# A chunked linear recurrence: the key product taken from the state two chunks back plus (k k') times the values between

## The chip, the core and the metric

The kernel runs on one NeuronCore of a Trainium2 chip. The metric is device time in microseconds from one launch to its end, the median of three runs. The profile shows one further execution. The engines are named as the profile names them: PE (matrix products), DVE (VectorE), ACT (ScalarE), POOL (GpSimd), SP (the DMA queue).

## The reference

A transformer layer on x of 2048 tokens and 512 features, all in fp32: a recurrent attention, then a gated FFN, each with a layernorm before and after and a residual sum. The recurrence has 16 heads of 32 and runs over 128 chunks of 16 tokens. Its state S is 32x32 for each head:

```
def step(S, (qi, ki, vi, ei)):                    # one chunk, all heads
    kh     = ki @ S
    mu, rstd = mean(kh), rsqrt(var(kh) + EPS);  kh_hat = (kh - mu) * rstd
    gw     = (w * kh_hat + b - (vi - ki)) * w
    v_new  = (gw - mean(gw) - kh_hat * mean(gw * kh_hat)) * rstd
    A      = tril(qi @ ki.T) * ei
    o      = qi + ln(qi @ S - A @ v_new)
    S      = S - (ki * ei).T @ v_new
    return S, o
```

Before it q = silu(x Wq), k = x Wk with each head's rows normalised, v = x Wv, e = 2 sigmoid(x Wbeta). After it o is gated with sigmoid(x Wg1 Wg2), normalised by head, and multiplied by Wo. The FFN has 1536 inner features; its weights are rounded to fp8 values inside the kernel.

What the change uses: with S_i = S_(i-1) - (k_(i-1) e_(i-1))' v_(i-1), the product k_i S_i is k_i S_(i-1) minus (k_i k_(i-1)') times (e v)_(i-1). The matrix k_i k_(i-1)' needs keys alone.

## The kernel before

**Blocks and steps.** The tokens are worked in 16 blocks of 128 (`NB`), each holding 8 chunks (`NC`) in two halves (`NHALF` = 4). The code counts blocks from 0.

**One step of the recurrence** (the function `chain`), for a chunk i of block b:

- PE, L768: `kh` = k·S, four matmuls whose weights are a spread copy of the keys, `kb` (each head's keys in its own rows and columns, zeros elsewhere), and whose data is `S`. In the trace each fp32 matmul appears as two passes, so a group of four is "x8".
- DVE, L772 to L782: products of `kh` with the rows of `row` (weights, targets) and their sums `z`, which hold mean and variance.
- ACT, L786: a square root. DVE, L790 to L815: a chain of small operations that makes factors and `m`. ACT, L801: part of the result, into a tile `up`'s bank (named u in the code).
- DVE, L821 and L824: `vb`, the new values times -e.
- PE, L832: `up` = `kr`' `vb`, the step of the state, with `kr` the keys in another layout that come back from memory.
- DVE, L840: `S` = `S` + `up`, into SBUF. Then the next step's L768.

Each `vb` also goes to memory (`give`), so that a whole block of values comes back as `vbt`.

**Around it.** For each block `pre` makes the layernorm, the transpose of x (`turned`), k (`product` with `wk_s`, L429, normalised by `head_rsqrt`), the transposed keys `kt` and the spread keys `kb` (L479, four copies on ACT of 32x512 from PSUM). `pre_v` makes v and the targets `tg` on POOL; they go through memory into `row`. `pre_sig` makes q (L583), the gate and beta with sigmoids on ACT (L591 to L599; a sigmoid and a square root need different tables, so that a table load stands between them). `scores` makes q k' (L634) and its mask (POOL, L647). `post` makes the output of a block from `S` of its start, the scores and `vbt`, and the product with `wo_s`. `weights` rounds the FFN's weights in 36 parts on DVE, POOL and ACT. All these are the side work of the recurrence. After its end the FFN runs (L978, L1007).

**The order.** `Sched` is a planner inside the kernel: each piece of work is a generator that yields the engine and the expected time of its next operation. The planner writes the operations out in the order in which they would run, the recurrence first, and lets a side operation stand ahead of a step of the recurrence only if by its costs it ends no later than `SLACK` after the step is due (`need`). On the chip each engine then runs its own list strictly in that order. The due times come from the list `steps`:

```
steps = [
    ("PE", 0.45), ("DVE", 0.4), ("DVE", 0.33), ("DVE", 0.47), ("ACT", 0.28, "sqrt"),
    ...
    ("PE", 0.66), ("DVE", 0.31),
]
```

Of the kernel before, what the change touches and what calls it, by code (L numbers as in the profile page):

```python
# [9 lines left out]
F32 = mybir.dt.float32  # L10
# [3 lines left out]
ALU = mybir.AluOpType  # L14
# [44 lines left out]
R_W = 1.0  # L59
R_PRE, R_SCO, R_POST = 0.0, 0.2, 1.4  # L60
# [20 lines left out]
class Sched:  # L81
# [62 lines left out]
    def run(self):  # L144
        while True:
# [13 lines left out]
            for eng in self.engine:  # L159
# [3 lines left out]
                    if t["chain"] or eng not in need or s + self._us(t) <= need[eng] + self.SLACK[eng]  # L163
# [17 lines left out]
def op(eng, us, need=None, late=0.0, table=None):  # L181
    return ("op", eng, us, need, late, table)
# [3 lines left out]
def kernel(  # L186
# [79 lines left out]
    with ExitStack() as st1:  # L266
# [42 lines left out]
        for n in range(2):  # L309
# [18 lines left out]
            zs.append(t)  # L328
        nums = p_kh.tile([P, D], F32, tag="kh", name="kh")
        kh = nums[:, 0 : 2 * DH].rearrange("p (r e) -> p r e", r=2)  # L330

# [4 lines left out]
        gen, tables = Slots(5), Slots(1)  # L336
# [11 lines left out]
        front = [Event() for _ in range(NB)]  # L348
        kr_in = [Event() for _ in range(2 * NB)]
        data = [{n: Event() for n in ("last_ot", "stored", "scored", "beta", "qt_in")} for _ in range(NB)]  # L350
# [14 lines left out]
        def head_rsqrt(src, scale, tag, newton=False):  # L365

            yield op("ACT", 0.65)
            sq = b2.tile([P, D], F32, tag="sq", name="sq")
            act(sq, src, AF.Square)
            yield op("DVE", 0.73)  # L370
            ss = small.tile([P, NH], F32, tag=tag + "s", name="ss")
            nc.vector.tensor_reduce(ss, by_head(sq), AX.X, ALU.add)
            if newton:
                return (yield from rsqrt_parts(ss, [P, NH], scale, 1e-6, small, tag + "n"))
# [33 lines left out]
        def turned(src, dst):  # L408

            yield ("take", gen, 1)  # L410
            yield op("PE", 0.6)
# [9 lines left out]
        def product(lhs, rhs, name):  # L421
# [3 lines left out]
            for k in range(4):  # L425
                yield op("PE", 1.0)
# [5 lines left out]
        def pre(b):  # L432
# [5 lines left out]
            if b >= 1:  # L438
                yield ("wait", front[b - 1])
# [6 lines left out]
            yield from turned(xn, xt)  # L446
            d["xt"] = xt
            got_k = Event()
            sched.add(pre_sig(b, xt), rank=b + R_PRE + 0.1)
# [22 lines left out]
            yield op("ACT", 0.65)  # L472
            kt = b2.tile([P, 4, P], F32, tag="kt", name="kt")
            nc.scalar.copy(kt, pt)
            d["kt"] = kt
            for h in range(4):
                end = yield op("ACT", 0.6)
                sl = slice(32 * h, 32 * h + 32)
                nc.scalar.copy(  # L479
                    kbs[b % 2][sl, :, :, h * CH : (h + 1) * CH].rearrange("p n g c -> p g n c"),  # L480
                    pt[sl].rearrange("p g (n c) -> p g n c", c=CH),
                )
            gen.put(end)
            ready[b].set(end)
            yield ("wait", d["stored"])
            yield ("wait", d["scored"])
            made[b].set(end)

# [15 lines left out]
        def pre_v(b, xt, got_k):  # L504
# [17 lines left out]
            m = small.tile([P, NH], F32, tag="tm", name="tm")  # L522
# [30 lines left out]
        def pre_sig(b, xt):  # L553
# [4 lines left out]
            for k in range(4):  # L558
                yield op("PE", 0.28)
                if pg is None:  # L560
                    pg = p_gen.tile([P, P], F32, tag="gen", name="pg")
                nc.tensor.matmul(pg[0:64, :], lhsT=wgb_s[:, k, :], rhs=xt[:, k, :], start=(k == 0), stop=(k == 3))
            end = yield op("ACT", 0.3)
            gb = b1.tile([64, P], F32, tag="gb", name="gb")
            nc.scalar.copy(gb, pg[0:64, :])
            gen.put(end)
            if b >= 1:
                yield ("wait", data[b - 1]["scored"])
            if b >= 3:
                yield ("wait", done[b - 3])  # L570
            yield ("take", gen, 3)
            yield op("PE", 0.28)
            pb = p_gen.tile([P, NH], F32, tag="gen", name="pb")
            nc.tensor.matmul(pb, lhsT=gb, rhs=bsel[0:64, :], start=True, stop=True)
            yield op("PE", 1.0)
            pgt = p_gen.tile([P, D], F32, tag="gen", name="pgt")
            nc.tensor.matmul(pgt, lhsT=gb, rhs=wg2_s, start=True, stop=True)
            pq = None
            for k in range(4):
                yield op("PE", 1.0)  # L580
# [4 lines left out]
            sb = b2.tile([P, NH], F32, tag="sb", name="sb")  # L585
# [4 lines left out]
            yield op("ACT", 0.65, table="sig")  # L590
            act(sg, pgt, AF.Sigmoid)  # L591
            end = yield op("ACT", 0.3, table="sig")
            act(sb, pb, AF.Sigmoid)
# [583 lines left out]
```

## Time and profile before

| | |
|---|---|
| median of 3 runs | 1137.34 us (1133.26 to 1147.24) |
| the profiled execution | 1126.66 us |
| its span | 1124.7 us |
| PE busy | 900.9 us, 80% |
| DVE busy | 709.5 us, 63% |
| ACT busy | 557.2 us, 50% |
| POOL busy | 462.4 us, 41% |
| PE's granted clock, mean | 0.838 |

How to read the profile's lines. A timeline line gives start and duration in us, the engine, the line of the kernel, the operation with output and inputs, and in brackets how long the engine stood idle before it and what ended that. PEld is PE's loading of weights, which overlaps its matmuls. A line by stretches gives the stretch and its length, then for PE, PEld, DVE, ACT and POOL the busy time and the number of instructions, then PE's granted clock as a share of full speed, the share of time that the DMA engines were busy, and GB/s. Buffer numbers are left out of names.

### The profile page before, as it was taken

The page shows a single profiled execution, that of the slowest core. Times are in us where ns is not written, and L with a number is a line of the kernel's source. Part 1 is how long each engine was busy: PE and PEld are TensorE (multiplying, and loading weights), DVE is VectorE, ACT ScalarE, POOL GpSimd, SP SyncE. Part 2 cuts the span into 40 slices and gives each one's busy share as a digit, 9 for nine tenths or more (in the row PEclk, how much of TensorE's full clock was granted, in tenths as well). Part 3 has the DMA queues.
Part 4 walks back from the last instruction along what each step waited for, and adds up shares of the span by engine and source line. Part 5 has one row for each costly group of instructions (what it writes and reads, how often), then busy time and mean ns, then how long its engine had stood idle before and what let it go on. Part 6 is the DMA issues. An engine that isn't in the chain of part 4 may idle for free. (4 is left out here: it accounts for less than half of the span.)

```text
span 1124.7 us, 17608 instructions
## 1 busy us (share of the span) xinstructions
PE 900.9 (80%) x5824; PEld 594.8 (53%) x5824; DVE 709.5 (63%) x2418; ACT 557.2 (50%) x1192; POOL 462.4 (41%) x380
## 2 busy tenths in 40 slices
PE   2868877877786877798877988766369999999996
PEld 1434544444443544454444544444236888888885
DVE  2266667667664757766767666676664666476635
ACT  1565546556564646757567575674232223233223
POOL 5543535556544635566545564464441001010011
PEclk9878667887877868886978869876579999999998
DMA  9323121221203222232222322215115001010000
GB/s 312 79 49 78 34 63 39 64 61 46 68 21 102 63 46 48 73 68 53 49 50 69 68 53 58 66 45 150 44 38 227 7 1 38 1 38 1 10 29 37
DMA packets 139370, 68.74 MB, mean 61 GB/s; under 512 B 106640, under 2 KB 119056, under 8 KB 139280
## 3 DMA queue, kind: packets, MB, share of 16 engines
q1 hardware_dynamic: 138256, 66.35, 22.2%
q0 software_dynamic: 272, 0.87, 0.3%
q8 instruction: 46, 0.75, 0.3%
q10 hardware_dynamic: 752, 0.40, 0.1%
q14 instruction: 44, 0.36, 0.1%
HBM read 41.25 MB, written 26.35 MB: 60 GB/s over the span
## 5 line engine op out<-in xcount | busy, mean ns | idle before, releaser
L832 PE MATMUL up<-vb,kr 64*128 64x32 f32 x1024 | 103.0, 313 | 114.8 <-DVE vb L824 72.2
L832 PEld LDWEIGHTS up<-vb,kr 64*128 64x128 f32 x1024 | 90.1, 226 | 178.4 <-ACT up L801 74.7
L978 PE MATMUL gu<-xh,w 128*128 128x512 f32 x384 | 153.2, 399 | 4.2 <-DVE sg L1026 2.4
L978 PE MATMUL gu<-xl,w 128*128 128x512 f32 x384 | 151.8, 395 | 0.0
L1080 POOL TENSOR_TENSOR y<-y,xa 128x512 f32<-128x512 f32 x15 | 19.3, 1288 | 244.9 <-ACT y L1074 171.2
L801 ACT ACTIVATE up<-row,k 128x32 f32<-128x32 f32 x256 | 97.3, 380 | 44.3 <-DVE k L806 28.5
L840 DVE TENSOR_TENSOR S<-S,up 128x128 f32<-128x128 f32 x128 | 36.8, 287 | 115.5 <-PE up L832 115.1
L786 ACT ACTIVATE sk<-z 128x2 f32<-128x2 f32 x128 | 26.0, 203 | 148.7 <-DVE z L782 148.2
L647 POOL TENSOR_TENSOR at<-at,cs 128x512 f32<-128x512 f32 x64 | 80.5, 1279 | 45.0 <-ACT at L640 45.0
L1007 PE MATMUL acc<-w,h 128*128 128x512 f32 x384 | 95.4, 391 | 0.4 <-DVE h L1037 0.2
L429 PE MATMUL pk<-wk_s,xt 128*128 128x512 f32 x128 | 87.9, 823 | 9.0 <-ACT at L640 9.0
L772 DVE TENSOR_TENSOR row<-kh,row 128x192 f32<-128x192 f32 x128 | 45.8, 358 | 71.7 <-PE kh L768 59.5
L768 PE MATMUL kh<-S,kb 128*64 128x32 f32 x1024 | 65.9, 251 | 30.2 <-DVE S L840 27.1
L881 POOL TENSOR_TENSOR raw<-raw,m 128x512 f32<-128x512 f32 x36 | 45.6, 1266 | 97.8 <-DVE m L878 89.9
L978 PEld LDWEIGHTS gu<-xh,w 128*128 128x128 f32 x384 | 73.3, 191 | 20.2 <-DVE sg L1026 2.8
L978 PEld LDWEIGHTS gu<-xl,w 128*128 128x128 f32 x384 | 73.2, 191 | 15.7 <-DVE xl L959 0.4
L1007 PEld LDWEIGHTS acc<-w,h 128*128 128x128 f32 x384 | 72.1, 188 | 16.2 <-ACT h L1035 0.6
L768 PEld LDWEIGHTS kh<-S,kb 128*64 128x64 f32 x1024 | 50.7, 163 | 51.2 <-DVE S L840 43.0
L583 PE MATMUL pq<-wq_s,xt 128*128 128x512 f32 x128 | 77.1, 735 | 0.0
L429 PE MATMUL po<-wo_s,ot 128*128 128x512 f32 x128 | 71.3, 695 | 2.9 <-ACT ot L417 2.9
L1035 ACT CAST h<-sg 128x512 fp32r<-128x512 f32 x48 | 29.9, 623 | 85.2 <-DVE sg L1029 76.7
L429 PE MATMUL pv<-wv_s,xt 128*128 128x512 f32 x128 | 68.1, 650 | 4.9 <-ACT xt L417 3.6
(183 smaller groups left out, 1876.9 us busy)
## 6 DMA issues: line engine op xcount, KB each, us to landing
w8d<-w SPq DMA_DIRECT2D x36, 256.0 KB
w<-w8d SPq DMA_DIRECT2D x12, 768.0 KB
tg_d<-tg SPq DMA_DIRECT2D x32, 132.0 KB
row<-tg_d SPq DMA_DIRECT2D x32, 132.0 KB
kc_d<-kn SPq DMA_DIRECT2D x16, 256.0 KB
kr<-kc_d SPq DMA_DIRECT2D x256, 16.0 KB
vb_d<-vb SPq DMA_DIRECT2D x128, 32.0 KB
vbt<-vb_d SPq DMA_DIRECT2D x16, 256.0 KB
```

The costliest lines, as they stand in the source:

```text
L429: nc.tensor.matmul(pp, lhsT=lhs[:, k, :], rhs=rhs[:, k, :], start=(k == 0), stop=(k == 3))
L583: nc.tensor.matmul(pq, lhsT=xt[:, k, :], rhs=wq_s[:, k, :], start=(k == 0), stop=(k == 3))
L647: gtt(view, view, causal.unsqueeze(1).to_broadcast([P, 4, P]), ALU.mult)
L768: nc.tensor.matmul(kh[half, g // 2, :], lhsT=kb[:, i, g, :], rhs=S[:, g, :], start=True, stop=True)
L772: tt(row[:, :, 3:6, 0:DH], kh.unsqueeze(2).to_broadcast([P, 2, 3, DH]), row[:, :, 0:3, 0:DH], ALU.mult,)
L801: act(u[:, r, :], row[:, r, 4, 0:DH], AF.Identity, bias=k1[:, 0, r : r + 1], scale=k1[:, 1, r : r + 1])
L832: nc.tensor.matmul(up[:, j, r * DH : r * DH + DH], lhsT=kr[half, ii, r, :], rhs=vb[half, r, :], start=True, stop=True,)
L840: tt(S2.rearrange("p (r j) e -> p r j e", r=2), S.rearrange("p (r j) e -> p r j e", r=2), up.rearrange("p j (r e) -> p r j e", r=2), ALU.add,)
L881: gtt(v, raw, m, ALU.add)
L978: nc.tensor.matmul(pp, lhsT=w[:, half, k * P : (k + 1) * P], rhs=part[:, k, :], start=(k == 0 and i == 0), stop=(k == 3 and i == 1),)
L1007: nc.tensor.matmul(accs[tb][s], lhsT=h[:, i, s * P : (s + 1) * P], rhs=w8[f][:, 2, :], start=(f == 0 and i == 0), stop=(f == NF - 1 and i ...
L1035: nc.scalar.copy(h[:, 0, :], sg)
```

## The change

The recurrence no longer needs the newest state for its product. For each pair of neighbouring chunks `gram` makes K = k_(i-1) k_i' from the spread keys (PE, L518, four matmuls a chunk, into one PSUM bank for half a block, copied to SBUF by ACT at L525). In a step k·S (`k_S`, L807) is issued with the state that lacks the newest `vb`, between `m` and `vb`, and leaves its sum open. When `vb` is there, K·vb (L910) is added in PSUM and closes the sum; then `up` (L922) follows. `up` is opened once and summed in PSUM over all 128 chunks, so DVE's sum L840 is gone; instead ACT copies the sum to SBUF as `S` once a step (L847), between `kh`'s first products and the square root.

The spread keys `kb` are written by POOL from `kt` (L491) and no longer by ACT from PSUM. The sigmoid of beta moves: a new `pre_beta` makes its argument early, and `pre_sig` takes block b+1's beta (and block 0's) with block b's gate and q in one run of sigmoids (L646 to L653); `over` lets such a run stand up to `OVER` = 3 us past a due time. Some buffers have one copy instead of two (`sq`, `o`), with slots that guard them. The planner's costs for PE are lower (a product's part 0.88 instead of 1.0), and `steps` holds written start times with a period of 3.94.

```diff
-def op(eng, us, need=None, late=0.0, table=None):
-    return ("op", eng, us, need, late, table)
+def op(eng, us, need=None, late=0.0, table=None, over=0.0):
+    return ("op", eng, us, need, late, table, over)
...
             for h in range(4):
-                end = yield op("ACT", 0.6)
+                end = yield op("POOL", 0.75)
                 sl = slice(32 * h, 32 * h + 32)
-                nc.scalar.copy(
+                nc.gpsimd.tensor_copy(
                     kbs[b % 2][sl, :, :, h * CH : (h + 1) * CH].rearrange("p n g c -> p g n c"),
-                    pt[sl].rearrange("p g (n c) -> p g n c", c=CH),
+                    kt[sl].rearrange("p g (n c) -> p g n c", c=CH),
                 )
...
+        def gram(b, half):
+            n = 2 * b + half
+            if n >= 2:
+                yield ("wait", gram_out[n - 2])
+            yield ("take", gen, 1)
+            pr = None
+            for i in range(NHALF * half, NHALF * half + NHALF):
+                if b == 0 and i == 0:
+                    continue
+                yield op("PE", 0.32)
+                if pr is None:
+                    pr = p_gen.tile([P, NHALF, 2, 64], F32, tag="gen", name="pr")
+                last = kbs[b % 2][:, i - 1] if i else kbs[(b - 1) % 2][:, NC - 1]
+                for g in range(4):
+                    at = slice(64 * (g % 2), 64 * (g % 2) + 64)
+                    nc.tensor.matmul(
+                        pr[at, i % NHALF, g // 2, :], lhsT=last[:, g, :], rhs=kbs[b % 2][:, i, g, :],
+                        start=True, stop=True,
+                    )
+            end = yield op("ACT", 0.65)
+            first = 1 if n == 0 else 0
+            t = b2.tile([P, NHALF, 2, 64], F32, tag="gram", name="gram")
+            nc.scalar.copy(t[:, first:], pr[:, first:])
+            gen.put(end)
+            grams[n % 2] = t
+            gram_in[n].set(end)
...
+            for n in nxt:
+                yield op("ACT", 0.25, table="sig", over=OVER)
+                act(data[n]["sb"], data[n]["sb"], AF.Sigmoid)
+            end = yield op("ACT", 0.65, table="sig", over=OVER)
             act(sg, pgt, AF.Sigmoid)
...
+        def k_S(b, i, S, stop):
+            for g in range(4):
+                half = slice(64 * (g % 2), 64 * (g % 2) + 64)
+                nc.tensor.matmul(
+                    kh[half, g // 2, :], lhsT=kbs[b % 2][:, i, g, :], rhs=S[:, g, :], start=(g < 2), stop=stop and g > 1,
+                )
...
+                    op_S = next(step)
+                    if b or i:
+                        yield ("at", t_up + HOP)
+                        yield op_S
+                        S = state.tile([P, 4, DH], F32, tag="S" if i else "S0", name="S")
+                        nc.scalar.copy(
+                            S.rearrange("p (r j) e -> p r j e", r=2), up.rearrange("p j (r e) -> p r j e", r=2),
+                        )
...
+                        yield ("wait", ready[nb])
+                        yield ("wait", gram_in[n2])
+                        yield op_K
+                        k_S(nb, ni, S, False)
...
+                    t_kh = yield next(step)
+                    for r in range(2):
+                        for j in range(2):
+                            half = slice(64 * j, 64 * j + 64)
+                            nc.tensor.matmul(
+                                kh[half, r, :], lhsT=grams[n2 % 2][half, ni % NHALF, r, :], rhs=vb[half, r, :],
+                                start=False, stop=(r == 1),
+                            )
...
                             nc.tensor.matmul(
                                 up[:, j, r * DH : r * DH + DH], lhsT=kr[half, ii, r, :], rhs=vb[half, r, :],
-                                start=True, stop=True,
+                                start=(b == 0 and i == 0 and r == 0), stop=(r == 1),
+                                skip_group_check=True,
                             )
...
-                    yield next(step)
-                    S2 = state.tile([P, 4, DH], F32, tag="S0" if i == NC - 1 else "S", name="S")
-                    tt(
-                        S2.rearrange("p (r j) e -> p r j e", r=2), S.rearrange("p (r j) e -> p r j e", r=2),
-                        up.rearrange("p j (r e) -> p r j e", r=2), ALU.add,
-                    )
-                    S = S2
```

## The prediction

> **What bounds the kernel now.** I read the granted clock first, then the busy time of each engine by stage, then single steps of the recurrence in the timeline. By stage the trace splits in three:
>
> ```profile
> core 0: us, PE busy (x) PEld busy (x) DVE busy (x) ACT busy (x) POOL busy (x), PEclk, DMA share, GB/s
> 52.00:810.00 758.00, 586.47 (x4415) 349.06 (x4413) 506.57 (x1968) 445.90 (x1012) 394.53 (x322) 0.78 0.25 60
> 810.00:837.00 27.00, 12.42 (x98) 7.11 (x96) 20.09 (x52) 7.44 (x14) 12.71 (x11) 0.69 0.15 41
> 837.00:1124.70 287.70, 275.91 (x1212) 225.19 (x1212) 170.37 (x355) 86.81 (x136) 26.50 (x21) 0.97 0.11 40
> ```
>
> The recurrence owns 758 of 1124.7 us and no engine is full in it: PE 77%, DVE 67%, ACT 59%, POOL 52%, PE's clock only 0.78 on average. The last stage is PE at full clock; the change does not touch it. So the recurrence is bound by its own round trip, 128 times. One step at full clock:
>
> ```profile
> 635.73 0.36 DVE L772 TENSOR_TENSOR row<-kh,row 128x192 f32<-128x192 f32 x1 [0.53 <-PE kh L768]
> ...
> 638.69 0.22 DVE L824 TENSOR_TENSOR vb<-m,up 128x64 f32<-128x64 f32 x1
> ...
> 639.06 0.64 PE L832 MATMUL up<-vb,kr 64*128 64x32 f32 x8 [0.60 <-ACT z L550]
> 639.73 0.29 DVE L840 TENSOR_TENSOR S<-S,up 128x128 f32<-128x128 f32 x1
> ...
> 640.07 0.42 PE L768 MATMUL kh<-S,kb 128*64 128x32 f32 x8
> 640.54 0.36 DVE L772 TENSOR_TENSOR row<-kh,row 128x192 f32<-128x192 f32 x1 [0.53 <-PE kh L768]
> ```
>
> and the same links at half clock:
>
> ```profile
> 803.25 0.22 DVE L824 TENSOR_TENSOR vb<-m,up 128x64 f32<-128x64 f32 x1
> ...
> 803.62 1.07 PE L832 MATMUL up<-vb,kr 64*128 64x32 f32 x8 [3.38 <-ACT m L886]
> 804.72 0.29 DVE L840 TENSOR_TENSOR S<-S,up 128x128 f32<-128x128 f32 x1 [1.25 <-PE up L832]
> ...
> 805.06 0.64 PE L768 MATMUL kh<-S,kb 128*64 128x32 f32 x8 [0.38 <-DVE S L840]
> 805.75 0.36 DVE L772 TENSOR_TENSOR row<-kh,row 128x192 f32<-128x192 f32 x1 [0.75 <-PE kh L768]
> ```
>
> Read each as three parts. A, from the start of `row` (L772) to the end of `vb` (L824): 3.18 us. B, on to the end of `S`: 1.11 us at full, 1.54 at half clock. C, on to the next `row`: 0.52 and 0.74. Over all starts of L772 in the timeline the step takes 5.93 us on average (753.7 us for 127): A 3.48, B 1.64, C 0.81. The floor at full clock is 3.15 + 1.11 + 0.53 = 4.79. The 1.14 us above it come from other work that stands in the way on PE, ACT and DVE, and from half clock, which by the 0.78 holds some 43% of the time (in half-microsecond slices the clock is nearly always 0.5 or 1).
>
> **The change on the round trip.** The new key product K·vb (L910) takes the place of `up`, the sum `S` and k·S after `vb`; k·S itself is issued before `vb` is there. A step is then A plus one matmul group. No row shows that group; the nearest is L768, also eight passes with 64 columns of weights and 32 of data (0.42 us), so its C holds: 0.53 full, 0.75 half clock. Floor: 3.15 + 0.53 = 3.68 us. B leaves the path: 1.1 to 1.5 us a step, 127 times, 140 to 195 us if nothing else were late. What is late next is PE.
>
> **PE's work.** Warm and cold unit times come from the issue intervals of the timeline: a 128x512 product k-step 0.87 and 1.72 us, a k·S group 0.31 and 0.51, an `up` group 0.50 and 0.96, a transpose group 0.46 and 0.80, 16 score or `qh` matmuls 0.9 to 1.8 and 1.6 to 2.0. New are, per chunk, K·vb (0.31 and 0.51) and the making of K (L518; nearest row k·S again, but 64 columns of data: between 0.31 and 0.5, I take 0.34; cold 0.60). With these I add up what PE's issue order holds between two chain groups. Before: 416 us at full clock for 127 steps, 3.28 a step. After: 495 us, 3.93 a step, more than the floor of 3.68. So PE and round trip are now about equal, and half the steps will be set by PE. The order also shows eight places near block ends where 5 to 17 us of other matmuls stand between `up` and the next k·S.
>
> The time of a step I take as the larger of round trip and PE work, at full clock and at half clock, weighted by their shares of time. The round trip is A's mean of 3.48 and the links. With 43% cold, the order of before gives 751 us against the 753.7 measured, so the method needs no correction. The order of after gives 728 us at 43% cold, 690 at 32% (clock 0.84), 648 at 20%, 787 at 60%, 579 with no cold time at all.
>
> **Which clock.** This is the largest choice. The trace:
>
> ```profile
> 478.00:486.00 8.00, 8.00 (x31) 4.68 (x31) 5.46 (x21) 3.36 (x10) 7.06 (x6) 0.50 0.12 31
> ```
>
> PE is busy all 8 us and still at half clock. The Trainium skill (TensorE: Matmul & The Clock Gate, Part 1: The HAM clock gate) says that about 3.4 us of sustained work release the full clock. By that rule the changed kernel, whose PE hardly pauses, runs at 1.0: 579 us. By this row a busy PE of small matmuls and waits is not enough, and the clock stays 0.78: 728 us. The row decides that the rule's "busy" is not the page's busy; but the work per time does rise, from 416/754 = 0.55 to about 0.7, which thins out the slack stretches that precede each drop. I take 0.84, 690 us: **-64 us**.
>
> **ACT.** It loses 64 `kb` copies (L479, 574 ns, 37 us) and, by the order, 28 of 60 table loads (1.283 us each, 36 us), since the sigmoids of two blocks stand together. It gains 127 copies of `S` from PSUM (nearest L474-like copies; 128 elements between 0.2 and 0.4, I take 0.29 as on DVE: 37 us), 32 copies of K (580 ns, 19 us). Net -17 us on an engine 59% busy. Two table loads around a sigmoid hold up the chain's square root (L786) by one to two microseconds; A's excess over 3.15 is 0.33 x 128 = 42 us in all. Half of the groups of loads go, each remaining one is longer: **-8 us** (bounds 0 and -20). The copy of `S` adds a wait: ACT stands until `up` is done, with the square root and both `up` activations (L801) behind it, and `m` waits for these. `up` ends about 0.6 us after `row` starts and the square root is wanted at 1.2, so 0.3 us are left after the copy at full clock; nearly nothing at half clock or with a transpose in between (45 of 127 steps have something there, 20 of them over 0.3 us). I cost it at nothing, bounds 0 and +35.
>
> **POOL and the block ends.** Spreading the keys moves from ACT to POOL, in order between its 1.27 us operations, and now ends in a PE group that waits for it, with the chain behind on PE. A one-input copy of 32x512 has no row: the memset of 128x2048 (1.825 us) scales to 0.46 for 512, the two-input L647 takes 1.27, the slowest, L304, 1.56. The Trainium skill (GPSIMD Engine Reference, 4.1 Engine selection) speaks against elementwise work there, but calls one-input work roughly line-rate. By that about the memset's pace, 64 x 0.5 = 32 us, by L647 81 us; I take 0.8, 51 us, which POOL can hold (395 + 51 of some 695). On the path are only the ends of blocks: four copies, K's making and its copy cost some 4 us instead of 2.3 us, and four blocks (8, 9, 10 and 15 of 0 to 15) have K directly ahead of its use: **+8 us** (0 to +45).
>
> **Start and end.** The first `row` waits for `tg` (L547's transfer, 5.8 us of idle DVE before it). The sigmoid in `tg` now waits for block 1's product and stands on ACT behind both copies of K: about 50 instead of 44 us, **+6 us** (0 to +10). Of the weight roundings one or two more parts remain after the last mask (POOL, 3.8 us each); the FFN needs them some 50 us later. SP's order is the same in kind. The end: no change.
>
> **Sum.** -64 - 8 + 8 + 6 = -58 us on 1126.66 (span 1124.7 plus 2): 1068.7. The median shown, 1137.34, lies 0.95% above the profiled execution; scaled, **1079 us**. About 2% is what a measurement of this kernel can tell from no change.
>
> **Rivals.**
> *Full clock* (0.15). The rule above holds: 10% cold gives about 613 us, total -135: 1001 us. For it: the last stage holds 0.97. Against: the row at 478.
> *Late keys* (0.17). POOL or the K groups hold up each block end by 2 to 3 us more, 15 times: +35, 1114 us. For it: one such stall of 9.4 us (the C ahead of block 6, blocks counted from 0) is in the trace already with ACT doing the copies. Against: POOL has 48% idle.
> *ACT couples the steps* (0.08). The wait for `up` delays the square root by 0.27 us a step: +35, 1114 us.
> *PE becomes the bound and stays cold* (0.10), the slower side. Place: PE's queue between `up` and k·S; price: 79 us more matmul at full clock, 133 at half clock. With the clock at 0.70 the sum is 787: +33 + 6 = +39, 1177 us. It decides from about 49% cold time (clock below 0.755), where the sum passes 748. For it: the added matmuls are all small, the kind present at half clock.
> That the change fails to shorten the path: K·vb waits, by the order, for `vb` alone within a half block; I give it no chance of its own.
>
> The forecast keeps 0.50, with its own range 1035 to 1112. Faster by over 2%: forecast, full clock and half of the two 1114 cases, 0.74; within: 0.19; slower: 0.07. The range that leaves out most of the cold case and the warmest end: 1018 to 1130.
>
> **What would show it.** Right: start to start of `row` near 5.4 us, K·vb to `row` 0.5 to 0.75, A still 3.4 to 3.6, PE busy over 85% and clock 0.80 to 0.88 in the recurrence, table loads 32 there, `kb` on POOL at 0.5 to 1.3 us, last stage 288 us. Wrong: A above 3.8 (ACT or DVE), stalls ahead of the K groups at block ends, or a clock at or below 0.76.

## The result and the profile after

The changed kernel takes **1138.74 us** (median of 20 executions, 1135.83 to 1142.35), the kernel before 1132.77 us, also of 20, in the same comparison: ratio 1.0051, 95% interval 1.0033 to 1.0070. It is half a per cent slower, where 1079 us and a gain of 5% were forecast.

The profiled execution spans 1138.6 us against 1124.7. By stage (the table of windows of the changed kernel: recurrence from the first to the last `row`, the stretch between, the last stage):

```profile
62.80:805.28 742.48, 640.14 (x6352) 402.23 (x6352) 470.54 (x1823) 408.75 (x1081) 418.61 (x369) 0.82 0.25 60
805.28:836.00 30.72, 13.61 (x104) 9.32 (x104) 27.17 (x71) 9.10 (x20) 17.83 (x14) 0.61 0.13 37
836.00:1138.60 302.60, 277.66 (x1212) 226.13 (x1212) 171.31 (x355) 89.80 (x141) 34.32 (x27) 0.96 0.11 41
```

The columns are, as before, length, then busy time of PE, PE's weight loads, DVE, ACT and POOL, then PE's clock. The recurrence gained 11.2 us (753.7 to 742.5). The first `row` starts 10.8 us later (62.8 instead of 52.0), and from the last `row` to the end it takes 14.4 us longer (333.3 instead of 319.0). The sum is the 13.9 us that the span grew.

The step itself became what the change intended. This is one at full clock (the timeline of the changed kernel; L833 is `row`, L807 k·S, L902 `vb`, L910 the new K·vb):

```profile
150.62 0.36 DVE L833 TENSOR_TENSOR row<-kh,row 128x192 f32<-128x192 f32 x1
...
153.30 0.42 PE L807 MATMUL kh<-S,kb 128*64 128x32 f32 x8 [0.99 <-ACT up L872]
...
153.61 0.22 DVE L902 TENSOR_TENSOR vb<-m,up 128x64 f32<-128x64 f32 x1
...
153.88 0.42 PE L910 MATMUL kh<-vb,gram 64*64 64x32 f32 x8 [0.15 <-DVE vb L902]
...
154.35 0.36 DVE L833 TENSOR_TENSOR row<-kh,row 128x192 f32<-128x192 f32 x1
```

k·S is done before `vb` is, and `row` follows `vb` by one matmul group: 3.73 us from `row` to `row`; the shortest step of the trace has 3.68. The median step fell from 5.62 to 4.86 us. But 7 of the 127 steps take 11 to 27 us, 135 us together, where before one took 14. All seven are the last step of a block of eight. This is the one at the end of block 9, 27.2 us (the same view; L885 is `m`, L485 `kt`, L491 the keys' copies, L518 the making of K, L899 and L902 the two adds that end in `vb`):

```profile
513.98 0.29 DVE L885 TENSOR_TENSOR m<-row,kh 128x128 f32<-128x128 f32 x1
...
517.59 0.57 ACT L485 COPY kt<-pt 128x512 f32<-128x512 f32 x1
...
527.92 3.72 POOL L702 TENSOR_TENSOR at<-at,cs 128x512 f32<-128x512 f32 x3 [0.18 <-ACT at L695]
531.60 1.23 POOL L758 TENSOR_TENSOR o<-o,r 128x512 f32<-128x512 f32 x1
532.77 2.75 POOL L491 COPY kb<-kt 32x512 f32<-32x512 f32 x4
...
535.58 0.45 PE L518 MATMUL pr<-kb,kb 128*64 128x64 f32 x8 [0.75 <-POOL kb L491]
...
537.82 0.21 DVE L899 TENSOR_TENSOR up<-m,up 128x64 f32<-128x64 f32 x1
538.07 0.22 DVE L902 TENSOR_TENSOR vb<-m,up 128x64 f32<-128x64 f32 x1
```

`m` is there at 514.3 and `vb`, two short adds later, at 538.3. In between every engine works through side operations. The four key copies were ready at 518.2 and ran at 532.8, behind masks and norms of other blocks; that looks like late keys, and the experiments had to tell whether it is.

The seven are not all held at the same place. In four, at the ends of blocks 2, 3, 11 and 14 (84 of the 135 us), `vb` and K·vb are done within 8 us of the step's `row`, and the next `row` waits: for the load of `tg`, and behind side operations on DVE. The one at the end of block 2, whose own `row` starts at 180.31:

```profile
184.95 0.42 PE L910 MATMUL kh<-vb,gram 64*64 64x32 f32 x8
...
203.78 1.98 SPq L588 DMA_DIRECT2D row<-tg_d  x2
...
207.50 0.36 DVE L833 TENSOR_TENSOR row<-kh,row 128x192 f32<-128x192 f32 x1 [5.05 <-DMA row<-tg_d]
```

The start, in the same view (L525 copies K, L646 is beta's sigmoid, L572 puts beta into `tg`, L588 loads `row`):

```profile
50.00 0.59 ACT L525 COPY gram<-pr 128x512 f32<-128x512 f32 x1 [0.45 <-PE pr L518]
50.59 1.28 ACT L646 ACT_TABLE_LOAD   x1
51.88 0.32 ACT L646 ACTIVATE sb<-sb 128x16 f32<-128x16 f32 x2
...
54.78 0.21 ACT L572 ACTIVATE tg<-sb 128x16 f32<-128x16 f32 x1
...
58.97 1.99 SPq L588 DMA_DIRECT2D row<-tg_d  x2
```

Beta of block 0 waits on ACT behind both copies of K; its column in `tg` is written at 54.8 instead of 44.2. The end, in the same view (the last part of the rounded weights on POOL and its store; then the FFN's cast L1119, its gate L1110 and its matmul L1062):

```profile
884.30 1.26 POOL L975 TENSOR_TENSOR w<-raw,m 128x512 fp32r<-128x512 f32 x1 [1.46 <-issue]
885.59 0.32 SPq L977 DMA_DIRECT2D w8d<-w  x1
...
887.79 0.62 ACT L1119 CAST h<-sg 128x512 fp32r<-128x512 f32 x1 [3.63 <-DMA w8d<-w]
...
889.05 0.75 DVE L1110 SCALAR_TENSOR_TENSOR sg<-gu,ps,sg 128x512 f32<-128x512 f32 x1
...
889.85 0.80 PE L1062 MATMUL gu<-xh,w 128*128 128x512 f32 x1 [12.54 <-DVE sg L1110]
```

The matmul waits for the gate on DVE, the gate for a sigmoid on ACT (L1107, at 888.32), and that stands in ACT's list behind the cast, which starts when the store of the last rounded weights has landed. So the late rounding holds the FFN through ACT's queue. Before, the last rounding on POOL ended at 853 us and the longest wait of PE in the last stage's first 160 us was 2.4 us.

### The profile page after: what moved, and what is told of

It is laid out like the page before. It is cut to its first block, busy times and chain, and to the rows that moved or that the text cites. A ratio compares the mean times of both kernels' runs of the same rounds, so it can differ in the third digit from the quotient of the medians.

```text
span 1138.6 us, 21826 instructions
## 1 busy us (share of the span) xinstructions
PE 964.3 (85%) x7848; PEld 655.1 (58%) x7848; DVE 681.0 (60%) x2290; ACT 524.9 (46%) x1275; POOL 502.4 (44%) x444
## 5 line engine op out<-in xcount | busy, mean ns | idle before, releaser
L1062 PE MATMUL gu<-xh,w 128*128 128x512 f32 x384 | 153.7, 400 | 13.8 <-DVE sg L1110 13.1
L1062 PE MATMUL gu<-xl,w 128*128 128x512 f32 x384 | 152.0, 396 | 2.4 <-DVE xl L1043 2.4
L833 DVE TENSOR_TENSOR row<-kh,row 128x192 f32<-128x192 f32 x128 | 45.9, 358 | 160.0 <-PE kh L910 132.9
L807 PEld LDWEIGHTS kh<-S,kb 128*64 128x64 f32 x1024 | 48.9, 156 | 119.9 <-ACT up L872 73.4
L847 ACT COPY S<-up 128x128 f32<-128x128 f32 x127 | 33.7, 265 | 171.4 <-PE up L922 137.5
L807 PE MATMUL kh<-S,kb 128*64 128x32 f32 x1024 | 62.2, 243 | 59.0 <-ACT up L872 29.4
L922 PE MATMUL up<-vb,kr 64*128 64x32 f32 x1016 | 96.6, 312 | 0.0
L1062 PEld LDWEIGHTS gu<-xh,w 128*128 128x128 f32 x384 | 73.5, 191 | 30.2 <-DVE sg L1110 13.9
L922 PEld LDWEIGHTS up<-vb,kr 64*128 64x128 f32 x1016 | 81.6, 223 | 11.8 <-issue 6.9
L1062 PEld LDWEIGHTS gu<-xl,w 128*128 128x128 f32 x384 | 73.5, 191 | 18.2 <-DVE xl L1043 2.9
L975 POOL TENSOR_TENSOR w<-raw,m 128x512 fp32r<-128x512 f32 x36 | 45.7, 1269 | 73.6 <-issue 52.4
L438 PE MATMUL po<-wo_s,ot 128*128 128x512 f32 x128 | 76.5, 730 | 0.2 <-ACT ot L426 0.2
L638 PE MATMUL pq<-wq_s,xt 128*128 128x512 f32 x128 | 74.5, 713 | 2.2 <-ACT at L695 2.2
L438 PE MATMUL pv<-wv_s,xt 128*128 128x512 f32 x128 | 72.4, 673 | 4.0 <-ACT xt L426 4.0
L438 PE MATMUL pk<-wk_s,xt 128*128 128x512 f32 x128 | 70.3, 671 | 0.0
L1119 ACT CAST h<-sg 128x512 fp32r<-128x512 f32 x48 | 29.8, 621 | 86.5 <-DVE sg L1113 80.0
```

What stands on the lines that cost most here:

```text
L438: nc.tensor.matmul(pp, lhsT=lhs[:, k, :], rhs=rhs[:, k, :], start=(k == 0), stop=(k == 3))
L638: nc.tensor.matmul(pq, lhsT=xt[:, k, :], rhs=wq_s[:, k, :], start=(k == 0), stop=(k == 3))
L807: nc.tensor.matmul(kh[half, g // 2, :], lhsT=kbs[b % 2][:, i, g, :], rhs=S[:, g, :], start=(g < 2), stop=stop and g > 1,)
L833: tt(row[:, :, 3:6, 0:DH], kh.unsqueeze(2).to_broadcast([P, 2, 3, DH]), row[:, :, 0:3, 0:DH], ALU.mult,)
L847: nc.scalar.copy(S.rearrange("p (r j) e -> p r j e", r=2), up.rearrange("p j (r e) -> p r j e", r=2),)
L922: nc.tensor.matmul(up[:, j, r * DH : r * DH + DH], lhsT=kr[half, ii, r, :], rhs=vb[half, r, :], start=(b == 0 and i == 0 and r == 0), stop ...
```

## The experiments

Theories: **T1**, the keys (POOL's copies, then K) come late. **T2**, beta and `tg` of the next block come late. **T3**, the order in the engines' queues holds the chain at block ends: side operations stand there, in order, ahead of the chain's next instruction. **T4**, behind T3: the shorter step leaves side work too little room under the planner's allowances (`SLACK`, how far a side operation may overrun the chain's due time), so it is put off until the chain stands still.

All runs at a glance, from the results and the profiled executions; each ratio is to the runs of before that stood beside it. "Rest" is from the last `row` to the end; the clock is PE's in the recurrence. The profile of pqcut is of its slowest execution (1146.68 us, median 1137.05), so its 750.1 is some 9 us long.

| kernel | median us | ratio to before (95%) | first `row` | recurrence | rest | steps over 10 us (sum) | mean of steps up to 7 us | clock |
|---|---|---|---|---|---|---|---|---|
| before | 1132.77 | 1 | 52.0 | 753.7 | 319.0 | 1 (14) | 5.66 | 0.79 |
| after | 1138.74 | 1.0051 (1.0033–1.0070) | 62.8 | 742.5 | 333.3 | 7 (135) | 4.81 | 0.82 |
| rows | 1123.53 | 0.9903 (0.9868–0.9938) | 62.7 | 723.4 | 332.3 | 6 (107) | 4.79 | 0.84 |
| keys | 1140.04 | 1.0061 (1.0041–1.0082) | 63.6 | 744.6 | 332.5 | 7 (135) | 4.82 | 0.82 |
| rowskeys | 1122.56 | 0.9891 (0.9842–0.9939) | 62.8 | 725.3 | 333.3 | 6 (105) | 4.76 | 0.83 |
| oldchain | 1162.22 | 1.0255 (1.0206–1.0303) | 60.0 | 780.3 | 319.5 | 0 | 5.83 | 0.75 |
| newchain | 1203.22 | 1.0616 (1.0547–1.0685) | 57.5 | 816.1 | 322.0 | 15 (278) | 4.60 | 0.79 |
| pqcut | 1137.05 | 1.0021 (1.0000–1.0042) | 62.1 | 750.1 | 332.6 | 8 (145) | 4.85 | 0.76 |
| noround | 1132.97 | 0.9985 (0.9957–1.0012) | 62.5 | 735.8 | 333.2 | 7 (132) | 4.82 | 0.82 |
| afterlean | 1071.80 | 0.9436 (0.9378–0.9494) | 61.5 | 653.0 | 360.8 | 3 (50) | 4.52 | 0.77 |
| beforelean | 1119.14 | 0.9846 (0.9793–0.9899) | 53.3 | 751.8 | 312.9 | 0 | 5.62 | 0.68 |
| slack6 | 1130.92 | 0.9978 (0.9959–0.9997) | 63.5 | 734.4 | 329.0 | 3 (53) | 5.12 | 0.83 |
| tuned1 | 1083.98 | 0.9534 (0.9478–0.9590) | 60.2 | 698.6 | 321.8 | 1 (13) | 5.15 | 0.85 |
| tuned2 | 1057.53 | 0.9310 (0.9252–0.9369) | 60.8 | 672.5 | 320.1 | 0 | 5.08 | 0.87 |
| b_t2 | 1176.69 | 1.0365 (1.0292–1.0438) | 52.6 | 807.8 | 315.2 | 2 (24) | 5.86 | 0.75 |
| t2_tight | 1130.62 | 0.9939 (0.9912–0.9965) | 61.4 | 738.6 | 329.4 | 6 (115) | 4.84 | 0.82 |
| allow | 1116.94 | 0.9845 (0.9787–0.9902) | 62.4 | 721.5 | 331.0 | 1 (10) | 5.11 | 0.83 |
| t2_kbact | 1154.56 | 1.0177 (1.0116–1.0239) | 61.0 | 776.8 | 317.1 | 5 (90) | 5.22 | 0.78 |
| t2_pqcut | 1056.55 | 0.9280 (0.9225–0.9336) | 61.2 | 673.5 | 320.1 | 0 | 5.12 | 0.83 |
| tuned3 | 1052.07 | 0.9239 (0.9171–0.9307) | 60.5 | 673.0 | 319.0 | 0 | 5.06 | 0.88 |

### Is it late data? rows, keys, rowskeys

The order of every queue is kept; only what the chain waits for is taken away.

```
# rows
-            dma(row.rearrange("p i r s e -> p (i r) s e")[:, :, 2, :], src[half])
+            b < 2 and dma(row.rearrange("p i r s e -> p (i r) s e")[:, :, 2, :], src[half])
# keys
-                nc.gpsimd.tensor_copy(
+                b < 2 and nc.gpsimd.tensor_copy(
# rowskeys: both
```

> The changed kernel in its own order; from block 2 on the transfer of tg into `row` (L588) is left out, so the chain works on the tg of an older block and no step waits for beta, tg or the two transfers behind them. Nothing else moves. Theory T2, the beta and tg of the next block come late: the 27 us step ahead of block 3, the 18 us step ahead of block 4 and the 22 us step ahead of block 15 go, 50 to 60 us less, near 1080 us. Theory T1, late keys: within 10 us of 1138. Theory T3, the queues themselves hold the chain at block ends because the planner found no hole for the side work during the steps and put it, in order, ahead of the chain's next instructions: at most 20 us less, 1118 or more.

> The changed kernel in its own order; from block 2 on the four POOL copies of the keys (L491) are left out, so k.S and the making of K work on keys of an older block and wait for no copy; POOL also has 36 us less to do. T1, late keys: the step ahead of block 10 (27 us) and parts of those ahead of 8, 9 and 15 go, 35 us or more less, near 1100 us. T2: within 10 us of 1138. T3: at most 15 us less, since POOL was 58% busy and the queues keep their order.

> Both cuts together: no step of the chain from block 2 on waits for anything that the next block's front part makes. If late data made the block-end stalls (T1 and T2), nearly all of the 100 us above an ordinary step go: 1040 to 1060 us. T3: the stalls stay in the queues, 1110 us or more.

Measured 1123.53, 1140.04 and 1122.56 us. The late `tg` is worth 15 us, the late keys nothing, both together 16 us. Of the 135 us in steps over 10 us, 105 remain although neither the next block's keys nor its `tg` can hold the chain any more. As a wait on the chip T1 falls; T2 holds for a small part, less than it expected. This is the step of the second timeline above in `rowskeys` (L638 is the q product, L662 multiplies it by its sigmoid, L412 and L414 are norm values of another block):

```profile
504.26 0.29 DVE L885 TENSOR_TENSOR m<-row,kh 128x128 f32<-128x128 f32 x1
...
515.91 5.40 PE L638 MATMUL pq<-wq_s,xt 128*128 128x512 f32 x8
...
522.08 0.68 DVE L662 TENSOR_TENSOR q<-pq,sgq 128x512 f32<-128x512 f32 x1
524.63 0.16 DVE L412 RECIPROCAL r<-z 128x1 f32<-128x1 f32 x1 [1.86 <-ACT z L408]
524.82 0.50 DVE L414 SCALAR_TENSOR_TENSOR nb<-mv,r 128x1 f32<-128x1 f32 x1
525.25 0.22 DVE L899 TENSOR_TENSOR up<-m,up 128x64 f32<-128x64 f32 x1
525.50 0.22 DVE L902 TENSOR_TENSOR vb<-m,up 128x64 f32<-128x64 f32 x1
```

Nothing that `vb` needs is missing after 504.6, but its two adds stand on DVE behind `q`, which waits for a sigmoid, which waits for `pq`, and behind `nb`, which waits for ACT. They run at 525.3. That is T3: the order holds the chain.

These runs keep the order of the queues, so they cannot say what made it. The kernel's text can. In `chain` the waits for the next block's keys and K (`ready`, `gram_in`) stand ahead of the two adds that end in `vb`, and the wait for its `tg` (`half_in`) ahead of `row`; while the planner has the recurrence stand at such a wait, nothing holds side operations back. The planner, run by itself from the text of the changed kernel, makes the same seven steps long, 122 us in the plan against 135 measured: at the ends of blocks 7, 8 and 9 it has the recurrence wait for keys or K (at the end of block 9 until 26.9 of the step's 27.9 us), at the ends of blocks 2, 3, 11 and 14 for `tg`. So the next block's data are late in the plan, in all seven, and the lists keep that shape even where the data are not awaited any more. A kernel with the waits for keys and K behind the adds of `vb` was not run.

### Which half of the change? oldchain, newchain

```
# oldchain: steps, chain_ops and chain as before the change; gram left out; all else as changed
# newchain: the changed chain, with
-                end = yield op("POOL", 0.75)
+                end = yield op("ACT", 0.6)
-                nc.gpsimd.tensor_copy(          # from kt
+                nc.scalar.copy(                 # from pt
-            nxt = ([0] if b == 0 else []) + ([b + 1] if b + 1 < NB else [])
+            nxt = [b]
-OVER, R_SIG = 3.0, 0.1
+OVER, R_SIG = 0.0, 0.1
# and the costs of PE's side work as before the change
```

> The changed kernel with the recurrence of before put back (up, sum S on DVE, k.S, then row; no K), and all else as changed: keys spread by POOL, beta bundled with the sigmoids of the block before, single buffers for the squares and o, the new costs. If the side changes cost time by themselves (the late start and late weights): 1140 to 1150 us, slower than before by what start and tail lost. If they gain through fewer table loads: 1110 to 1125 us. If they do nothing: 1133.

> The changed recurrence (K and the open sum) with the side changes undone: keys spread by ACT from PSUM, each block's beta in its own run of sigmoids with no allowance to overrun, the old costs of PE's side work. If the side changes were what spoiled the gain (late keys on POOL, late beta): under 1110 us. If they were needed to make room on ACT for the faster steps: above 1140 us.

oldchain takes 1162.22 us, slower than any of its three forecasts; newchain takes 1203.22, on the side of "needed to make room". The side changes alone cost 29 us, though not where I had put it: only the start is late (60.0), the end is as before (319.5), and the recurrence lost 27 us in steps of 5.83 instead of 5.66 us. The chain alone has the shortest ordinary steps of the kernels that keep all the work, 4.60 us, and a step of 15 to 25 us at each of the 15 block ends. In its trace the first `row` of every block from 1 on starts within 0.2 us of the copy that ends the load of `tg` (L591): there T2 holds throughout. So with the faster chain the side changes, taken together, are worth 64 us; they were not what spoiled it. Which of them does it (early beta, POOL's keys, the sigmoids' allowance, the new costs) these two runs do not separate.

### Less work in the same order: pqcut, noround

```
# pqcut
-                nc.tensor.matmul(pq, lhsT=xt[:, k, :], rhs=wq_s[:, k, :], start=(k == 0), stop=(k == 3))
+                (b and k) or nc.tensor.matmul(pq, lhsT=xt[:, k, :], rhs=wq_s[:, k, :], start=(k == 0), stop=(b > 0 or k == 3))
# noround: "f < 9 or" ahead of the two ts, the first two gtt and the two act of a weight part; the last gtt adds v to v there
```

> The changed kernel in its own order; from block 1 on the q product keeps one of its four matmul steps (L638), so PE has 45 steps of 0.87 us less, 39 us at full clock, 48 at the clock of 0.82. If PE's work now bounds the recurrence: 40 to 50 us less, near 1092 us. If the chain of side operations at block ends bounds it (each waits for the one before on another engine), only what of pq stands in those stalls counts: 10 to 20 us less, 1120 us or more.

> The changed kernel in its own order; for 27 of the 36 parts of the FFN weights the rounding is left out but for its last POOL operation: 69 us less on POOL, some 30 us each less on ACT and DVE, nothing on PE. If PE bounds the recurrence: within 6 us of 1138. If ACT, DVE and POOL queues hold the chain and the side operations: 20 us less or more, under 1118 us.

pqcut: 1137.05 us, the same as after (1138.74) within the intervals. The windows of pqcut:

```profile
62.13:812.27 750.14, 627.26 (x6262) 409.07 (x6262) 470.96 (x1823) 409.09 (x1081) 418.46 (x369) 0.76 0.25 59
```

PE's busy time fell by 13 us, not by 39, as its clock fell from 0.82 to 0.76; the recurrence did not get shorter. Whether PE's work is no bound here, or the lower clock takes the saving back, this run alone does not tell. noround took 76 us from POOL, 30 from ACT and 36 from DVE in the recurrence and gained 6 us (1132.97). Both gains are below what was expected if the queues hold the chain (10 to 20 us, and 20 or more), and noround's is what was expected if PE bounds it. What speaks for the order is that the large steps stay where less work is in the same queues: 145 and 132 us of them, 135 in the changed kernel.

### Room beside the chain: afterlean, beforelean

```
# both, in scores(b) and post(b), from block 2 on
+            if b >= 2:
+                at_in[b].set(t)      # scores, masks left out
+                return
...
+            if b >= 2:
+                at_out[b].set(t)     # qh, norms, output product left out
+                ...
+                return
```

> The changed kernel, planned anew, with the scores, masks and the whole of `post` (qh, norms, output product) left out from block 2 on, so that the steps have about a third less side work beside them. If the side work's pace sets the blocks (T4: the chain outruns the front part and waits for it at block ends), the big steps go, and the recurrence falls from 742 to about 620 us, near 1010 us in all. If the chain's own links set it: the recurrence stays above 690 us, near 1090 us.

> The same cut in the kernel before. T4: its steps were near their own round trip already, so the cut brings less: the recurrence falls from 754 to about 690 us, near 1065 us, and the changed kernel with the same cut is faster than it by 40 us or more. If the changed chain gains nothing even with room beside it: the two come out within 15 us.

The signs are as T4 expects, the sizes are not. With the room, the changed kernel's recurrence falls to 653.0 us (50 us of it are three large steps, at the ends of blocks 0, 2 and 3), 1071.80 in all; the kernel before stays at 751.8. The changed one is faster by 47 us. Both expected totals were too low, by 62 and 54 us. Of the 62, 33 are the recurrence and 28 lie behind it, where PE stands still for 57.7 us until the last weights are rounded and stored. In both kernels PE's clock fell with its work, to 0.77 and 0.68. That fits the kernel before standing still: its round trip has two matmul groups on it, `up` and k·S, which take longer at the lower clock.

### The order: slack6, tuned1, tuned2

The planner's numbers are changed, and in the sets also which block's beta shares which run of sigmoids; the work is the same. The sets for tuned1 and tuned2 (and tuned3 below) were chosen by the order that the planner lays out while the program is built: few large gaps in the chain.

```
# slack6
-    SLACK = {"PE": 0.3, "DVE": 0.3, "ACT": 0.35, ...
+    SLACK = {"PE": 0.3, "DVE": 0.6, "ACT": 0.35, ...
# tuned2 (tuned1: SLACK 0.4, 0.7, 0.35; OVER, R_SIG = 2.5, 0.1; R_SCO, R_POST = -0.5, 2.0)
-    SLACK = {"PE": 0.3, "DVE": 0.3, "ACT": 0.35, ...
+    SLACK = {"PE": 0.4, "DVE": 0.7, "ACT": 0.6, ...
-R_W = 1.0
+R_W = -1
-OVER, R_SIG = 3.0, 0.1
+OVER, R_SIG = 2, -0.5
-R_PRE, R_SCO, R_POST = 0.0, 0.2, 1.4
+R_PRE, R_SCO, R_POST = 0.0, 0.2, 1.7
-            nxt = ([0] if b == 0 else []) + ([b + 1] if b + 1 < NB else [])
+            nxt = [0] if b == 0 else [1, 2] if b == 1 else [b + 1] if b + 1 < NB else []
-                yield ("rank", 1.3 * f + R_W)
+                yield ("rank", 1.0 * f + R_W)
```

> The changed kernel with one number of the planner changed: a side instruction may overrun the chain's due time on DVE by 0.6 us instead of 0.3. The same work in another order. T3: side work gets into the steps, a step grows by some 0.2 us, and the large steps at block ends shrink to a third: 40 to 60 us less, near 1090 us. T1 and T2 (the data take their time whatever the order): within 10 us of 1138.

> The changed kernel, all work kept, with the planner's numbers set for the shorter step: allowances of 0.4 us on PE, 0.7 on DVE, 0.35 on ACT, 2.5 for the sigmoids, other ranks for scores, post and weights, and the beta of block 0 in a run of sigmoids of its own. T4: the same side work, spread over the steps, fills them to about 5 us each with few large steps, first row near 53 us, no late weights: the total falls by 40 to 55 us, to 1083 to 1098 us. If the front part's data or PE's work bound the blocks: within 15 us of 1138.

> A second such set (0.4 on PE, 0.7 on DVE, 0.6 on ACT, 2.0 for the sigmoids), whose order repeats from block to block. T4: no step over 10 us at a block end, steps of 5.1 us on average at full clock, 1088 to 1105 us. Otherwise within 15 us of 1138.

slack6 behaved as T4 says in kind (large steps from 135 to 53 us, ordinary ones from 4.81 to 5.12) but gained 8 us, not 40 to 60: one number trades the one loss for the other. The sets gained much more: 1083.98 us, as expected, and **1057.53 us**, below what was expected. tuned2 has the same matmuls as after and the same side work, but for four more table loads on ACT (39 instead of 35):

```profile
60.82:733.37 672.55, 612.47 (x6352) 390.72 (x6350) 464.05 (x1827) 415.14 (x1085) 421.43 (x375) 0.87 0.29 67
```

The recurrence is 70 us shorter than after and 81 us shorter than before, with no step over 10 us; the end is as before (320.1), without that wait. The first `row` is still late (60.8): the early beta of block 0 did not mend the start. From the trace, blocks 7 to 13 have the same pattern of steps and take 39.4 to 41.9 us each, 47 before.

### Which numbers, and only for this chain? allow, t2_tight, b_t2

```
# allow: after, with SLACK 0.4, 0.7, 0.6 alone
# t2_tight: tuned2, with SLACK 0.3, 0.3, 0.35 again
# b_t2: before, with tuned2's SLACK, R_POST and ranks of the weights
```

> The changed kernel with the three allowances alone (0.4, 0.7, 0.6). If they carry the gain: at most two steps over 10 us, recurrence near 680 us, 1070 to 1095 us, the late start and the late weights still there. If not: 1125 us or more.

> The second set with the three allowances put back to 0.3, 0.3 and 0.35, all else of the set kept. If the allowances carry the gain: large steps at block ends again, 110 us or more of them, 1115 to 1140 us. If the ranks and the early beta carry it: within 15 us of 1057.

> The kernel before with the second set's numbers (allowances 0.4 on PE, 0.7 on DVE, 0.6 on ACT, the same ranks of post and weights). If the set helps any order: 1060 to 1110 us. If it helps only because the changed step leaves smaller holes, while the steps of before already had room for 0.7 us operations: no gain, the allowances only lengthen its steps, 1135 to 1160 us.

Without the allowances the large steps are back (115 us) and the time is 1130.62, as expected. The allowances alone remove all but one large step, yet give 1116.94 us and not 1070 to 1095. So they are needed and not enough: alone they bring 22 us, the rest of the set 8, together 81. Every set makes a new order as a whole; which part of the rest does it was not separated. allow keeps 25 steps over 7 us (200 us) where tuned2 has 9 (73 us), and its clock is 0.83 and not 0.87. In the kernel before the same numbers cost 3.65% (1176.69 us, above the 1135 to 1160 expected): the set fits the changed step and not the old one. No other set was tried in the kernel before, so what tuning would bring there is open.

### Keys by POOL, PE's work, and a third set: t2_kbact, t2_pqcut, tuned3

```
# t2_kbact: tuned2, keys copied by ACT from pt as in newchain
# t2_pqcut: tuned2, with pqcut's edit
# tuned3: tuned2, with SLACK 0.3, 0.65, 0.6; OVER 2.5; R_W = 0
```

> The second set with the keys spread by ACT from PSUM again instead of POOL: ACT has 64 copies of 574 ns more, 37 us, POOL 39 us less. If ACT's holes are what is short: 1085 us or more. If POOL's copies delay the making of K at block ends: 1057 us or less.

> The second set in its own order, with three of the four matmul steps of the q product left out from block 1 on: 39 us less of PE work at full clock, 45 at its clock of 0.87. If PE's work bounds it: 1010 to 1025 us. If the clock gives the saving back, as it did in the order with the stalls: within 10 us of 1057. If the order of DVE and ACT binds: 1040 to 1057 us with the clock unchanged.

> A third set: allowances 0.3 us on PE, 0.65 on DVE, 0.6 on ACT, 2.5 for the sigmoids, rank of the weights 0 in place of -1, all else as in the second. If any order without large block-end steps has the gain: 1045 to 1085 us. If the second set's order was a lucky one: above 1095 us.

Keys on ACT cost 97 us (1154.56): the large steps return. Part of that may be the new order that any edit brings; the size says that room on ACT is short and POOL's copies are a gain. t2_pqcut gives 1056.55, no change, and its windows show where the saving went:

```profile
61.18:734.65 673.47, 586.72 (x6261) 390.53 (x6260) 466.93 (x1828) 415.33 (x1085) 420.89 (x376) 0.83 0.28 67
```

PE is busy 26 us less, the clock is 0.83 instead of 0.87, the length is the same. tuned3 gives **1052.07 us**, 7.6% less than before (ratio 0.9239, 0.9171 to 0.9307): the gain is not one order's luck. It is the version of this study to keep; its 7.6% are against a kernel before whose own numbers were left as they were.

## Why the prediction was wrong, step by step

**The round trip: right.** Floor 3.68 us forecast, shortest step 3.68 measured. A, from `row` to `vb`, is 3.48 us on average over the 119 of 127 steps where it stays under 5 us, the number used; over all 127 it is 3.82 (before: 3.48), which the prediction had named as a sign of being wrong (above 3.8). 23 of the 44 us between the two are the step at the end of block 9. The three links left the path. Start to start was forecast near 5.4 us; the median is 4.86 and the mean 5.85, so the ordinary steps came out better than forecast and a few far worse.

**PE's work and the clock: half right.** The clock was taken as 0.84 and came out 0.82, inside the 0.80 to 0.88 named. At 0.82 the prediction's own table lies between its 690 (0.84, 32% cold) and 728 (43%): 36% cold gives about 704 us. So 14 us of the miss are the clock. The choice of 0.84 between the two was a guess, and that it came close is partly luck. The term is also built wrongly: it treats PE work as a bound and the clock as given. pqcut and t2_pqcut took 39 us of that work away and neither recurrence got shorter; the clock fell instead. (A slip without weight: 495 us over 127 steps is 3.90 a step, not 3.93.)

**ACT: right in sum.** The copy of `S` (265 ns each) did not couple the steps: A stayed 3.48 outside the eight long cases, and that rival, 0.27 us in every step, falls. Of the table loads half are gone: 33 instead of 61 up to 806 us. The 8 us forecast for them do not show in A either; whether they and a small cost of the copy cancel was not separated.

**POOL and the block ends: this step failed.** A key copy took 613 ns (0.8 was taken), as these two groups of the changed kernel show (busy time and mean ns of one behind the bar):

```profile
L491 POOL COPY kb<-kt 32x512 f32<-32x512 f32 x64 | 39.2, 613 | 33.6 <-ACT kt L485 31.5
...
L847 ACT COPY S<-up 128x128 f32<-128x128 f32 x127 | 33.7, 265 | 171.4 <-PE up L922 137.5 <-issue 18.2 <-DVE kh L864 4.2
```

But the block ends cost about 100 us, and the term for them was 8 (0 to 45): seven steps of 135 us, less seven ordinary ones of 5.06 (the mean of the other 120). The prediction asked how long the keys take after `kt`. The question was what stands in the queues between two instructions of the chain, keys, `tg` and all the side work that is laid there while the plan waits for them. It had the evidence: "eight places near block ends where 5 to 17 us of other matmuls stand between `up` and the next k·S". These were counted as PE time, so a part of the 100 us was in the forecast already. They were the places where the planner, finding no room for side work beside steps of 3.94 us, had let the chain stand, on all engines at once: the runs with wider allowances take them away. What the sum lacked is the time in these steps in which PE, too, waits: some 33 us, by its busy share in each. With the 704 us above that leaves 5 us of the 742.5 unexplained.

**Start and end.** The start lost 10.8 us where 6 were forecast (0 to 10); 0.96 of it is there at the first matmul already, before anything that the change touches. The end lost 14.4 us where nothing was forecast. Two more parts remained after the last `row`, as forecast (5 instead of 3), but the FFN could not spare the time: the last part was rounded 80 us after the last `row`, before 47, and PE stood still for 12.5 us.

**The sum.** Forecast -58, measured +14 on the span: 72 us apart, of which 14 are the clock, 39 the rest of the recurrence, 5 the start, 14 the end.

**The rivals.** Late keys had the place of three of the seven steps and the wrong mechanism: without the copies nothing changed on the chip; it is the plan that waits for keys, and in the other four steps for `tg`. Full clock did not come in any run (0.88 at most in the recurrence). "PE becomes the bound and stays cold" needed a clock below 0.755; it was 0.82. (The chance of "faster", 0.74, adds up to 0.775 by the shares named.) That the planner's numbers no longer fit the step was not among the rivals, and it is what decided: after and tuned3 run the same number of instructions on every engine and take 1139 and 1052 us by their order.

## What to carry to other kernels

When a loop's step gets shorter, look for the work that used to run in its gaps: count the gaps that each side operation still fits into, and reset the scheduler's allowances before judging the change. Read the distribution of the steps, not their mean: a median that falls by 0.76 us beside a sum that hardly moves says that the gain was handed to a few large steps. The plan showed them before any run, 122 us in the seven steps of 135; ask there what the loop is made to wait for. Placing a wait later in the loop's list, behind the instructions that do not need it, is a remedy that this study did not try. A saving on an engine whose clock follows its load may not be one; test it by leaving the work out.

## What the runs showed of the hardware

PE's clock followed its load in four pairs of kernels. Less matmul work lowered the clock. In the first three pairs the recurrence stayed as long as it was. In the fourth it got shorter; there, as in the third, the scores, masks and `post` are left out, which takes work from every engine:

| pair | PE busy us | clock | recurrence us |
|---|---|---|---|
| after, pqcut | 640.1, 627.3 | 0.82, 0.76 | 742.5, 750.1 |
| tuned2, t2_pqcut | 612.5, 586.7 | 0.87, 0.83 | 672.5, 673.5 |
| before, beforelean | 585.5, 498.8 | 0.79, 0.68 | 753.7, 751.8 |
| after, afterlean | 640.1, 541.1 | 0.82, 0.77 | 742.5, 653.0 |

How the clock moves can be read from the clock records of the traces. It stands at half or full and changes at multiples of 3.41 us. In the recurrence of the kernel before, PE was busy at least 96% of the 3.41 us ahead of every rise to full clock (27 of them) and at most 81% ahead of every drop (28, 52% on average); in the changed kernel at least 94% (21 rises) and at most 77% (21 drops). But being busy is not enough: of the 37 stretches of 3.41 us at half clock in which PE was busy 99% or more, 11 brought no rise in the kernel before, and 18 of 37 in the changed one. The 8 us at 478 that the prediction shows hold one such stretch, and behind it one that ends with a rise (kernel before, by stretches):

```profile
479.99:483.41 3.42, 3.42 (x14) 1.62 (x13) 1.96 (x9) 1.93 (x6) 2.56 (x3) 0.50 0.10 16
483.41:486.82 3.41, 3.41 (x18) 2.43 (x17) 2.33 (x12) 1.07 (x4) 3.33 (x4) 0.50 0.22 73
486.82:490.24 3.42, 3.00 (x26) 1.80 (x25) 1.09 (x6) 2.74 (x6) 1.71 (x2) 1.00 0.36 56
```

The Trainium skill (TensorE: Matmul & The Clock Gate, Part 1: The HAM clock gate) says that the gate is set by how busy PE has been recently; the direction agrees. Its rule that some 3.4 us of sustained work give the full clock agrees with what stands ahead of each rise, but, taken as enough, it would have had the changed recurrence, with PE busy 86% of the time, run near 1.0; measured was 0.82. What keeps the clock at half after a busy stretch, no run here shows.
